# Moving the layer-norm preparation of the later MLP batches one chunk ahead of the matrix work (one core, 16 batches)

## The chip, the cores and the metric

The kernel runs on one core of a Trainium2 chip. The metric is the device time of one execution in microseconds; lower is better. The engines go by the profile's names: PE (matmuls) with PEld (its weight loads), DVE (vector), ACT (scalar, activations), POOL (GpSimd) and SP (which here only issues DMAs, one after the other in the order written).

## The reference, cut to what matters

A transformer block over 16 batches of 256 tokens with 256 features: self-attention, cross-attention, and then, for each batch, the MLP part, which is all that the change touches:

```
x_norm2 = modulate(_ln(x), shift_m, scale_m)     # _ln: over the 256 features of a token
h = jax.nn.gelu(x_norm2 @ W_mlp1 + b_mlp1)       # 256 -> 1024
h = h @ W_mlp2 + b_mlp2                          # 1024 -> 256
x = x + gate_m[:, None] * h
```

## The kernel before, in words

The attention of all batches runs first (some 560 us) and writes its result to a DRAM tensor `x2d`. Then a loop runs over `chunks`: 16 batches b with 4 chunks c each, i = 4b + c. A chunk is 256 of the 1024 hidden features. All matrix products are three fp32r matmuls in place of one (high part and low part of each factor), so a chunk is 12 matmuls into the hidden layer (`mlp_first`, PSUM tile `ph`) and 12 out of it (`mlp_second`, into the PSUM tiles `s` for even batches and `st` for odd ones).

In iteration i the PE does `mlp_first` of chunk i+2 and then `mlp_second` of chunk i-1. Between the two, ACT applies the gelu to chunk i+1 (`mlp_gelu`: twice `hf` and twice `hh`, from `ph`), and POOL subtracts (`hl` = `hf` - `hh`). There are two PSUM buffers for `ph`. So `mlp_first` of chunk i+2 cannot start before the gelu of chunk i has read its `ph`.

What a batch m needs before its own first chunk is prepared while earlier batches compute, in these steps:

1. `mlp_load(m)`: SP reads x of the batch from `x2d` (a DMA of 256 KB).
2. `mlp_bias(m)`: POOL adds a bias row, x <- x, cb.
3. `mlp_stats(m)`: DVE `BATCH_NORM_STATS2` (`st_m`) and aggregate (`mv_m`); `ln.pow()`: POOL makes the reciprocal deviation, two small instructions on `rs_m`.
4. `mlp_apply(m)`: DVE normalises in two instructions (`xn_m`) and transposes in blocks (`blk_m`); SP writes the blocks to a DRAM tensor `turned` in 4 DMAs.
5. `mlp_fetch(m)`: SP reads them back, regrouped, into `raw_m` in 4 DMAs, which wait for the 4 writes.
6. `mlp_T(m)`: ACT scales and shifts (`xTf_m` from `raw_m`, two instructions), POOL splits the result into a high part (a cast into `wkch` or `wqch`) and a low part (`wkcl` or `wqcl`). With that, `mlp_first(m, 0)` can run.

DVE also does the end of each batch: `mt` (PSUM times gate, waits for the last `mlp_second` of the batch), `y` (plus residual) and, a little earlier, `xmg`.

What sets the order: PE, DVE, POOL and SP keep the order in which the program is written. ACT keeps it only in the iterations i < 23; behind them (`ACT.on` is False) a scheduler, which works with estimated durations when the kernel is built, chooses the place of each ACT instruction. That concerns `xTf_m` from batch 7 on: it is written in iteration (m-1, 0), behind that iteration's gelu, but the scheduler puts it earlier. In the trace each engine runs its list in order, so an `xTf_m` that waits for its read back holds every gelu behind it.

Of the kernel before, what the change touches and what calls it, by code (L numbers as in the profile page):

```python
# [21 lines left out]
def pixart_block(  # L22
# [8 lines left out]
    B, N, H = x.shape  # L31
# [69 lines left out]
    def tok(ap, b):  # L101
        return ap[b].rearrange("(p t) h -> p t h", p=P)
# [329 lines left out]
    def mm3_tok(dst, xT, t, W, kn=KC, start=True, stop=True):  # L432
        n = 0
        for k in range(kn):
            for a, b in ((xT[0], W[0]), (xT[0], W[1]), (xT[1], W[0])):
                PE.matmul(dst, a[:, k, t * P:(t + 1) * P], b[:, k],
                          start=(start and n == 0), stop=(stop and n == 3 * kn - 1))
                n += 1
# [134 lines left out]
    def bc_t(ap):  # L573
        return ap.unsqueeze(1).to_broadcast([P, NT, H])
# [113 lines left out]
    def side(home, r):  # L688
        return home[r] if isinstance(home, (list, tuple)) else home[:, r]
# [111 lines left out]
    M = {}  # L801
# [9 lines left out]
    def mlp_bias(b):  # L811
        POOL.tensor_tensor(M[b].xt, M[b].xt, bc_t(cb), ALU.add)

    def mlp_stats(b, power=False):
        M[b].ln.steps[0]()
        M[b].ln.steps[1](power)

    BY_DVE = range(3, B)
    turned = dram.tile([2, 32, 16, 4, 32], F32, name="turned", bufs=1)

    def mlp_apply(b):
        m = M[b]
        if b not in BY_DVE:
            m.ln.steps[2]("dve")
            return
        xn = work.tile([P, 4, KC, NT, 32], F32, tag="xn", name=f"xn_m{b}", bufs=3)
        for t in range(NT):
            DVE.tensor_scalar(xn[:, :, :, t], m.xt[:, t].rearrange("p (f g c) -> p g f c", f=KC, g=4),
                              m.ln.mv[:, t, 0:1], m.ln.rs[:, t:t + 1], ALU.subtract, ALU.mult)
        blocks = work.tile([P, 4, KC * NT, 32], F32, tag="A", name=f"blk_m{b}", bufs=1)  # L830
        DVE.transpose(blocks.rearrange("p g x c -> p (g x c)"), xn.rearrange("p g f t c -> p (g f t c)"))
        home = turned[b % 2]
        for i in range(4):
            SP.dma_start(home[:, :, i], blocks[32 * i:32 * i + 32].rearrange("p g x c -> p (g x) c"))

    def mlp_fetch(b):
        m, home = M[b], turned[b % 2]
        m.raw = work.tile([P, KC, N], F32, tag="oT", name=f"raw_m{b}")
        for g in range(4):
            SP.dma_start(m.raw[32 * g:32 * g + 32].rearrange("p f n -> p (f n)"),  # L840
                         home[:, 4 * g:4 * g + 4].rearrange("a x i c -> a (x i c)"))
# [7 lines left out]
    def mlp_residual(b):  # L849
        m = M[b]  # L850
        m.xg = work.tile([P, NT, H], F32, tag="x1", name=f"xmg_{b}", bufs=7)
        DVE.tensor_tensor(m.xg, m.xt, bc_t(m.g[:, 1]), ALU.add)

    def mlp_T(b):

        m = M[b]
        raw = b in BY_DVE
        pst = m.raw.rearrange("p f n -> p (f n)") if raw else ps_gen(f"psT_m{b}", SHORT)
        for f in range(0 if raw else KC):
            for t in range(NT):  # L860
                PE.transpose(pst[:, f * N + t * P:f * N + (t + 1) * P],
                             m.ln.xn[:, t, f * P:(f + 1) * P], ident)
        y = work.tile([P, KC, N], F32, tag="y", name=f"xTf_m{b}", bufs=2)
        hi, lo = (Wkc, Wqc)[b % 2]
        if raw:
            for f in range(KC):
                ACT.activation(y[:, f], m.raw[:, f], AF.Identity,
                               bias=cpT[:, 6 + f, b:b + 1], scale=sc1[:, 1, f, b:b + 1])
            POOL.tensor_copy(hi, y)
            POOL.tensor_tensor(lo, y, hi, ALU.subtract)  # L870
            m.xT = (hi, lo)
            return
        for f in range(KC):
            DVE.tensor_scalar(y[:, f], pst[:, f * N:(f + 1) * N], sc1[:, 1, f, b:b + 1],
                              cpT[:, 6 + f, b:b + 1], ALU.mult, ALU.add)
        if b in E_['DV']:
            DVE.tensor_copy(hi, y)
        else:
            for f in range(KC):
                ACT.activation(hi[:, f], pst[:, f * N:(f + 1) * N], AF.Identity,  # L880
                               bias=cpT[:, 6 + f, b:b + 1], scale=sc1[:, 1, f, b:b + 1])
        DVE.tensor_tensor(lo, y, hi, ALU.subtract)
        m.xT = (hi, lo)
# [3 lines left out]
    def mlp_first(b, c):  # L887

        ph = ps_gen(f"ph_{b}_{c}", LONG).rearrange("p (j n) -> p j n", j=2)
        for j in range(2):  # L890
            mm3(ph[:, j], W1, 2 * c + j, M[b].xT)
        M[b].h[c] = ph
# [27 lines left out]
    def mlp_gelu(b, c):  # L920
        ph = M[b].h.pop(c)
        homes = (("pt", 5), ("qkh", 3), ("qkl", 3))
        if b == 0 and c:
            homes = (("x1", 7),) + (homes[1:] if c < 3 else (("xTh", 5), ("xTl", 5)))
        hf, hh, hl = [work.tile([P, 2, N], t, tag=tag, name=f"{n}_{b}_{c}", bufs=bufs)
                      for n, t, (tag, bufs) in zip(("hf", "hh", "hl"), (F32, F32R, F32R), homes)]
        for dst in (hf, hh):
            if c in M[b].kept:
                ACT.activation(dst, ph, AF.Gelu_apprx_tanh)
                continue  # L930
            for j in range(2):
                f = BM1 + 2 * c + j
                ACT.activation(dst[:, j], ph[:, j], AF.Gelu_apprx_tanh, bias=bT[:, f:f + 1])
        POOL.tensor_tensor(hl, hf, hh, ALU.subtract)
        M[b].hT[c] = (hh, hl)

    def mlp_second(b, c):
        m = M[b]
        hT = m.hT.pop(c)
        if c == 0:  # L940
            m.po = [side((sp, st)[b % 2], t)[:, :H] for t in range(NT)]
            if b == B - 1:
                m.po[1] = side(sp, 1)[:, :H]
        for t in range(NT):
            mm3_tok(m.po[t], hT, t, [W2[0][:, 2 * c:2 * c + 2], W2[1][:, 2 * c:2 * c + 2]],
                    kn=2, start=(c == 0), stop=(c == NCH - 1))
        if c == NCH - 1:
            t1 = work.tile([P, NT, H], F32, tag="t1", name=f"mt_{b}")
            y = work.tile([P, NT, H], F32, tag="x1", name=f"y_{b}", bufs=7)
            if b < B - 1:  # L950
                for t in range(NT):
                    DVE.tensor_tensor(t1[:, t], m.po[t], m.g[:, 0], ALU.mult)
                DVE.tensor_tensor(y, m.xg, t1, ALU.add)
                SP.dma_start(tok(out, b), y)
                return
            for t, q in enumerate((SP, ACT)):
                DVE.tensor_tensor(t1[:, t], m.po[t], m.g[:, 0], ALU.mult)
                DVE.tensor_tensor(y[:, t], m.xg[:, t], t1[:, t], ALU.add)
                q.dma_start(tok(out, b)[:, t], y[:, t])
# [106 lines left out]
    for i in range(3):  # L1066
        b = i if i < 2 else 0
# [191 lines left out]
    for i, (b, c) in enumerate(chunks):  # L1259
        ACT.on = i < E_['AP']  # L1260
        if 2 < i < len(chunks) - 1:
            mlp_gelu(*chunks[i + 1])
        if i in turns:
            mlp_T(turns[i])
        if c == 3 and b > 0 and b + 3 in BY_DVE:
            mlp_apply(b + 3)
        if c == 0 and b > 1 and b + 2 in BY_DVE:
            mlp_fetch(b + 2)
        if i in firsts:
            mlp_first(*chunks[firsts[i]])  # L1270
        if i > 0:
            mlp_second(*chunks[i - 1])
        for f in pst.get(i, ()):
            f()
        ahead = b + 2 if 2 < b + 2 < B else None
        soon = ahead if ahead and ahead in BY_DVE else None
        if c == 0 and ahead and not soon:
            mlp_bias(ahead)
        if c == 0 and b > 0 and b + 3 in BY_DVE:
            mlp_bias(b + 3)  # L1280
        if c == 1:
            if b + 1 < B:
                mlp_gates(b + 1)
            if b > 0 and b + 3 in BY_DVE:
                mlp_stats(b + 3)
                M[b + 3].ln.pow()
            if ahead and not soon:
                mlp_stats(ahead)
        if c == 2 and ahead and not soon:
            M[ahead].ln.pow()  # L1290
        if c == 0 and 4 < b + 4 < B:
            mlp_load(b + 4)
        if c == 3:
            if ahead and not soon:
                mlp_apply(ahead)
            mlp_residual(b)
    mlp_second(*chunks[-1])


# [46 lines left out]
```

## Time and profile before

| | |
|---|---|
| median of 3 runs | 736.87 us (735.96 to 737.25) |
| the profiled execution | 736.51 us, of which the span (first to last instruction) is 734.7 us |
| PE busy | 727.2 us, 99% of the span |
| DVE, ACT, POOL busy | 565.7, 562.8 and 521.5 us |
| granted PE clock | 0.999 on average |
| DMA queue of SP | 92.27 MB, 45.5% of 16 engines |

The MLP loop fills the last 170 us or so, from about 560 us on. In it the PE works through 12 matmuls in about 1.42 us, an iteration in 2.83 us and a batch in 11.33 us, as long as nothing makes it wait. Batch numbers in the trace follow from that raster: iteration (4, 0) starts at about 594.6 us, iteration (8, 0) at 640.88 us. The changes begin in iteration (2, 3), about 583 us.

### The profile page before, as it was taken

The numbers are of one execution on the slowest core, as the hardware profiler recorded it, in microseconds if no ns is written. First come the engines' busy times: TensorE is split into PE (matmuls) and PEld (weight loads), VectorE is DVE, ScalarE is ACT, GpSimd is POOL, SyncE is SP. The second block draws the span as 40 slices with busy tenths as digits, with TensorE's granted clock in tenths as the row PEclk, the third lists the DMA queues.
The fourth block names the chain that finished last, engine by engine and source line by source line (L and its number), as shares of the span: only waits on it lengthen the run. The fifth ranks groups of instructions, "written<-read, shape, count | busy, mean of one in ns | idle before, by whom it ended". The sixth has DMA issues, their size and how long they took to land.

```text
span 734.7 us, 25385 instructions
## 1 busy us (share of the span) xinstructions
PE 727.2 (99%) x10092; PEld 642.2 (87%) x10092; DVE 565.7 (77%) x1164; ACT 562.8 (77%) x976; POOL 521.5 (71%) x638
## 2 busy tenths in 40 slices
PE   9999999999999999999999999999999999999997
PEld 9778888888888888888888888888889999999997
DVE  4888888988888888988888889888746765556542
ACT  4277898888888888888888888888887666666663
POOL 6757576858567575856757687888576888898873
PEclk9999999999999999999999999999999999999999
DMA  6755444543545454354545456454321644444421
GB/s 209 203 149 146 130 134 137 141 125 96 154 115 155 131 142 136 107 152 114 159 125 143 137 145 161 124 158 129 117 74 36 164 133 113 112 124 100 116 80 37
DMA packets 108906, 94.81 MB, mean 129 GB/s; under 512 B 36914, under 2 KB 92756, under 8 KB 108788
## 3 DMA queue, kind: packets, MB, share of 16 engines
q1 hardware_dynamic: 108308, 92.27, 45.5%
q8 instruction: 80, 1.31, 0.8%
q0 software_dynamic: 192, 0.52, 0.3%
q10 hardware_dynamic: 288, 0.39, 0.2%
q14 instruction: 38, 0.31, 0.1%
HBM read 30.38 MB, written 11.86 MB: 57 GB/s over the span
## 4 chain that ended last, share of the span: by engine, by line
PE 90%; POOL 2%; DVE 2%; issue 2%; ACT 2%; DMA 1%; SPq 1%; ACTq 0%; POOLq 0%; DVEq 0%
PE s L51 17%; PE o L51 16%; PE st L51 14%; PE ph L51 8%; PE ps_q L51 5%; PE ps_qc L51 5%; PE ps_kc L51 4%; PE ps_P_s L51 3%; PE ps_v_c L51 3%; PE ps_k L51 3%; PE ps_v_s L51 2%; PE ps_P_c L51 2%; PE ps_h L51 1%; PE psT_q L51 1%; PE psA_c L51 1%
## 5 line engine op out<-in xcount | busy, mean ns | idle before, releaser
L51 DVE TENSOR_REDUCE mx<-s 128x2 f32<-128x512 f32 x504 | 324.4, 683 | 64.1 <-PE s L51 57.0
L51 ACT ACTIVATE pt<-st 128x1024 f32<-128x1024 f32 x252 | 259.0, 1028 | 16.6 <-PE st L51 10.8
L51 PE MATMUL s<-big 63*128 63x256 f32 (+1 forms) x1024 | 183.5, 297 | 0.2 <-DVE mx L51 0.2
L51 PEld LDWEIGHTS s<-big 63*128 63x128 f32 (+1 forms) x1024 | 133.2, 185 | 19.0 <-DVE l_kc L51 6.6
L51 PE MATMUL st<-big 64*128 64x256 f32 (+1 forms) x1024 | 133.8, 298 | 0.3 <-ACT pt L51 0.2
L51 PE MATMUL o<-pt,v 128*32 128x256 f32 x2048 | 123.8, 382 | 0.0
L51 PEld LDWEIGHTS st<-big 64*128 64x128 f32 (+1 forms) x1024 | 95.5, 185 | 16.2 <-issue 12.9
L51 POOL TENSOR_TENSOR hl<-hf,hh 128x512 fp32r<-128x512 f32 x64 | 85.4, 1342 | 32.3 <-ACT hh L51 31.9
L51 PEld LDWEIGHTS o<-pt,v 128*32 128x32 f32 x2048 | 60.2, 109 | 41.4 <-PE psm L51 0.2
L51 ACT ACTIVATE hh<-ph,bT 128x256 fp32r<-128x256 f32 x114 | 47.9, 472 | 23.2 <-PE s L51 10.9
L51 ACT ACTIVATE hf<-ph,bT 128x256 f32<-128x256 f32 x114 | 47.6, 471 | 21.6 <-PE ph L51 21.5
L51 ACT COPY oT<-o 128x512 f32<-128x512 f32 x63 | 37.0, 587 | 33.5 <-PE o L51 33.5
L51 PE MATMUL s<-big,hh 128*128 128x256 f32 x272 | 49.8, 282 | 0.0
L51 PE MATMUL ph<-wkch,wself 128*128 128x256 f32 x224 | 44.5, 282 | 0.5 <-ACT hh L51 0.4
L51 PE MATMUL ph<-wqch,wself 128*128 128x256 f32 x224 | 44.3, 281 | 0.0
L51 PE MATMUL ps_k<-xTh_s,wself 64*128 64x256 f32 (+1 forms) x232 | 43.9, 294 | 0.0
L51 PE MATMUL st<-big,hh 128*128 128x256 f32 x240 | 43.8, 281 | 0.0
L51 DVE TENSOR_SCALAR xn_m<-x,mv_m,rs_m 128x256 f32<-128x256 f32 x28 | 28.7, 1066 | 19.1 <-POOL rs_m L51 19.1
L51 POOL CAST xTh_c<-y_c 128x512 fp32r<-128x512 f32 x16 | 9.8, 613 | 45.5 <-ACT y_c L51 45.5
L51 PEld LDWEIGHTS s<-big,hh 128*128 128x128 f32 x272 | 41.4, 188 | 0.0
L51 PE MATMUL ps_q<-xTh_s,wself 64*128 64x256 f32 (+1 forms) x240 | 39.8, 283 | 0.4 <-DVE l_q L51 0.4
L51 PE MATMUL ps_v_s<-wself,xTh_s 64*128 64x256 f32 x224 | 39.2, 294 | 0.0
(249 smaller groups left out, 2496.1 us busy)
## 6 DMA issues: line engine op xcount, KB each, us to landing
big<-h_kc SPq DMA_DIRECT2D x64, 128.0 KB
big<-h_qc SPq DMA_DIRECT2D x64, 128.0 KB
big<-h_k SPq DMA_DIRECT2D x62, 128.0 KB
big<-h_q SPq DMA_DIRECT2D x62, 128.0 KB
big<-l_k SPq DMA_DIRECT2D x32, 128.0 KB
big<-l_q SPq DMA_DIRECT2D x32, 128.0 KB
g<-gd SPq DMA_DIRECT2D x16, 256.0 KB
c<-in_ctx_dram SPq DMA_DIRECT2D x16, 256.0 KB
```

What stands on the lines that cost most here:

```text
L51: i = f(*a, **k)
```

## The change

For batches m of 6 and above, four steps are written earlier:

| step | before, in iteration | now, in iteration |
|---|---|---|
| `mlp_bias(m)` | (m-3, 0) | (m-4, 3), at its end |
| `mlp_stats(m)` and `ln.pow()` | (m-3, 1) | (m-3, 0) |
| `mlp_apply(m)` | (m-3, 3) | (m-3, 2) |
| `mlp_fetch(m)` | (m-2, 0) | (m-3, 3) |

Nothing is added or removed, and `mlp_load` and `mlp_T` stay where they were written.

```diff
-        if c == 3 and b > 0 and b + 3 in BY_DVE:
+        if b > 0 and b + 3 in BY_DVE and c == (2 if b + 3 >= 6 else 3):
             mlp_apply(b + 3)
-        if c == 0 and b > 1 and b + 2 in BY_DVE:
+        if c == 3 and 6 <= b + 3 < B:
+            mlp_fetch(b + 3)
+        if c == 0 and 3 < b + 2 < 6:
             mlp_fetch(b + 2)
...
-        if c == 0 and b > 0 and b + 3 in BY_DVE:
+        if c == 0 and 3 < b + 3 < 6:
             mlp_bias(b + 3)
+        if c == 0 and 6 <= b + 3 < B:
+            mlp_stats(b + 3)
+            M[b + 3].ln.pow()
         if c == 1:
...
-            if b > 0 and b + 3 in BY_DVE:
+            if 3 < b + 3 < 6:
                 mlp_stats(b + 3)
                 M[b + 3].ln.pow()
...
             mlp_residual(b)
+            if 6 <= b + 4 < B:
+                mlp_bias(b + 4)
```

What it does to the engines' lists is seen in two places; the lists of DVE, SP and PE hold the same instructions in the same order as before.

ACT, around the last gelus of batch 5 (`hf_5_3` is the gelu of batch 5, chunk 3; `xTf_m7` belongs to `mlp_T(7)`), before:

```order
L51 ACTIVATE xTf_m6_13173<-raw_m6_13005,cpT_101,sc1_103 128x256 x2
L51 ACTIVATE hf_5_2_13217<-ph_5_2_13183,bT_104 128x256 x2
L51 ACTIVATE hh_5_2_13218<-ph_5_2_13183,bT_104 128x256 x2
L51 ACTIVATE hf_5_3_13261<-ph_5_3_13225,bT_104 128x256 x2
L51 ACTIVATE hh_5_3_13262<-ph_5_3_13225,bT_104 128x256 x2
L51 ACTIVATE xTf_m7_13346<-raw_m7_13178,cpT_101,sc1_103 128x256 x2
L51 ACTIVATE hf_6_0_13294<-ph_6_0_13269,bT_104 128x256 x2
L51 ACTIVATE hh_6_0_13295<-ph_6_0_13269,bT_104 128x256 x2
```

and now:

```order
L51 ACTIVATE xTf_m6_13179<-raw_m6_12965,cpT_101,sc1_103 128x256 x2
L51 ACTIVATE hf_5_2_13226<-ph_5_2_13184,bT_104 128x256 x2
L51 ACTIVATE hh_5_2_13227<-ph_5_2_13184,bT_104 128x256 x2
L51 ACTIVATE xTf_m7_13352<-raw_m7_13138,cpT_101,sc1_103 128x256 x2
L51 ACTIVATE hf_5_3_13261<-ph_5_3_13234,bT_104 128x256 x2
L51 ACTIVATE hh_5_3_13262<-ph_5_3_13234,bT_104 128x256 x2
L51 ACTIVATE hf_6_0_13303<-ph_6_0_13278,bT_104 128x256 x2
L51 ACTIVATE hh_6_0_13304<-ph_6_0_13278,bT_104 128x256 x2
```

The scheduler has put `xTf_m7` one gelu earlier, ahead of chunk 3 of batch 5 in place of chunk 0 of batch 6. The same holds for batches 8 to 15, nine in all; `xTf_m6` stays where it was.

POOL, in batch 6 (`x2_9` is the bias sum of batch 9, `rs_m9` its deviation), before:

```order
L51 TENSOR_TENSOR hl_6_0_13296<-hf_6_0_13294,hh_6_0_13295 128x512
L51 TENSOR_TENSOR hl_6_1_13340<-hf_6_1_13338,hh_6_1_13339 128x512
L51 CAST wqch_93<-xTf_m7_13346 128x512
L51 TENSOR_TENSOR wqcl_94<-xTf_m7_13346,wqch_93 128x512
L51 TENSOR_TENSOR x2_9_13215<-x2_9_13215,cb_106 128x512
L51 TENSOR_TENSOR hl_6_2_13392<-hf_6_2_13390,hh_6_2_13391 128x512
L51 TENSOR_SCALAR rs_m9_13431<-mv_m9_13428 128x2
L51 TENSOR_TENSOR rs_m9_13431<-rs_m9_13431,mhalf_73 128x2
L51 TENSOR_TENSOR hl_6_3_13436<-hf_6_3_13434,hh_6_3_13435 128x512
```

and now:

```order
L51 TENSOR_TENSOR hl_6_0_13305<-hf_6_0_13303,hh_6_0_13304 128x512
L51 TENSOR_TENSOR x2_9_13224<-x2_9_13224,cb_106 128x512
L51 TENSOR_TENSOR hl_6_1_13346<-hf_6_1_13344,hh_6_1_13345 128x512
L51 CAST wqch_93<-xTf_m7_13352 128x512
L51 TENSOR_TENSOR wqcl_94<-xTf_m7_13352,wqch_93 128x512
L51 TENSOR_SCALAR rs_m9_13394<-mv_m9_13391 128x2
L51 TENSOR_TENSOR rs_m9_13394<-rs_m9_13394,mhalf_73 128x2
L51 TENSOR_TENSOR hl_6_2_13401<-hf_6_2_13399,hh_6_2_13400 128x512
L51 TENSOR_TENSOR hl_6_3_13436<-hf_6_3_13434,hh_6_3_13435 128x512
```

The bias sum has moved from behind the split of batch 7 to ahead of `hl_6_1`, and the two `rs` instructions from behind `hl_6_2` to ahead of it.

## The prediction

> **What bounds the kernel now.** First the page's span and the busy time by stretches (columns: length, then busy time and count for PE, PEld, DVE, ACT and POOL, then granted clock, DMA share, GB/s), for the part in which the change acts:
>
> ```profile
> span 734.7 us, 25385 instructions
> ...
> core 0: us, PE busy (x) PEld busy (x) DVE busy (x) ACT busy (x) POOL busy (x), PEclk, DMA share, GB/s
> 580.00:600.00 20.00, 20.00 (x172) 20.00 (x171) 13.29 (x18) 13.56 (x33) 17.47 (x16) 1.00 0.51 129
> 600.00:620.00 20.00, 19.59 (x166) 19.39 (x165) 11.13 (x19) 12.86 (x32) 15.85 (x16) 1.00 0.48 130
> 640.00:660.00 20.00, 19.89 (x169) 19.69 (x167) 11.00 (x20) 13.33 (x34) 17.30 (x16) 1.00 0.45 117
> 660.00:680.00 20.00, 20.00 (x172) 20.00 (x171) 11.73 (x18) 13.84 (x34) 16.85 (x16) 1.00 0.42 105
> 720.00:734.70 14.70, 10.41 (x89) 10.20 (x87) 4.85 (x8) 4.20 (x10) 3.98 (x3) 0.94 0.11 38
> ```
>
> PE sets the pace: 172 matmuls in 20 us, one each 0.1163 us (0.118 by the raster of single rows). It loses time in two stretches only: 6 matmuls at 600 to 620 (0.70 us) and 3 at 640 to 660 (0.35 us), together 1.05 us. That is all that removing waits can bring. Then the waits from 580 to 720 (total, times, longest):
>
> ```profile
> DVE st_m L51 <- POOL x L51: 11.9, 10, 1.2
> ACT xTf_m L51 <- DMA raw_m<-turned: 11.1, 8, 2.7
> ...
> PEld ph L51 <- ACT hh L51: 0.9, 2, 0.6
> ```
>
> DVE's statistics wait 1.19 us in each batch for POOL's bias sum; ACT's `xTf_m` waits for the read back; and twice that reaches PE through `hh`. The first of these cases, batch 7, in the order in which the rows release each other (start, duration):
>
> ```profile
> 597.64 0.75 DVE L51 TENSOR_TENSOR mt<-st,gm 128x256 f32<-128x256 f32 x2 [1.65 <-PE st L51]
> 598.43 1.20 DVE L51 TENSOR_TENSOR y<-xmg,mt 128x512 f32<-128x512 f32 x1
> ...
> 599.05 1.73 POOL L51 TENSOR_TENSOR x<-x,cb 128x512 f32<-128x512 f32 x1
> ...
> 600.81 0.75 DVE L51 BATCH_NORM_STATS2 st_m<-x 128x6 f32<-128x256 f32 x2 [1.18 <-POOL x L51]
> ...
> 602.41 0.72 POOL L51 TENSOR_TENSOR rs_m<-rs_m,mhalf 128x2 f32<-128x2 f32 x1
> 603.10 2.61 POOL L51 TENSOR_TENSOR hl<-hf,hh 128x512 fp32r<-128x512 f32 x2
> ...
> 603.17 2.69 DVE L51 TENSOR_SCALAR xn_m<-x,mv_m,rs_m 128x256 f32<-128x256 f32 x2 [1.39 <-POOL rs_m L51]
> 605.89 0.71 DVE L51 STREAM_TRANSPOSE blk_m<-xn_m 128x512 f32<-128x512 f32 x1
> ...
> 606.63 2.57 SPq L51 DMA_DIRECT2D turned<-blk_m  x4
> ...
> 615.25 1.10 ACT L51 ACTIVATE xTf_m<-raw_m,cpT,sc 128x256 f32<-128x256 f32 x2 [2.66 <-DMA raw_m<-turned]
> ...
> 616.97 0.83 ACT L51 ACTIVATE hh<-ph,bT 128x256 fp32r<-128x256 f32 x2
> ...
> 617.85 0.38 PE L51 MATMUL ph<-wkch,wself 128*128 128x256 f32 x1 [0.41 <-ACT hh L51]
> ```
>
> The chain starts with `mt`, which PE releases at the end of batch 3, and ends 17.61 us later, when the read back lands and `xTf_m7` starts. From there to the released matmul it is 617.85 - 615.25 = 2.60 us (`xTf`, `hf`, `hh`). PE needs that gelu, chunk 0 of batch 6, for the matmuls of iteration (6, 0). `mt` starts 0.20 us behind the end of iteration (4, 0) on the raster, and seven iterations of 2.833 us (24 matmuls) lie between: 19.83 - 0.20 = 19.63 us. So the read back may land at most 19.63 - 2.60 = 17.03 us after `mt`. It was late by 0.58 us, and the matmul at 617.85 is 0.57 us behind the raster. The model holds to 0.01 us here.
>
> **The change, part by part.**
>
> 1. The bias sum ahead of `hl_1` takes away DVE's wait: statistics, deviation, normalising, write and read back come 1.19 us sooner. DVE and SP keep their lists, so moving `mlp_stats`, `mlp_apply` and `mlp_fetch` in the program does nothing more there: the next wait in line is `y`, then the DMAs' own time.
>
> 2. ACT's list is the cost. From batch 7 to 15 `xTf_m` stands one gelu earlier. The gelu now held up is chunk 3 of batch m-2, needed by PE one iteration, 2.83 us, sooner. The limit falls from 17.03 to 14.20 us, while the data gain 1.19 us.
>
> 3. The two `rs` ahead of `hl_2` let two `hl` run back to back while DVE normalises. With two, `xn` takes 2.69 us (above); with one:
>
> ```profile
> 649.62 1.29 POOL L51 TENSOR_TENSOR hl<-hf,hh 128x512 fp32r<-128x512 f32 x1
> ...
> 649.70 1.70 DVE L51 TENSOR_SCALAR xn_m<-x,mv_m,rs_m 128x256 f32<-128x256 f32 x2 [1.39 <-POOL rs_m L51]
> ```
>
> So it is 1 us (2.67 is the usual long value, I take 0.97) more where the second `hl` is ready in time: `hl_2` and `hl_3` now, the latter only if its gelu wasn't late, which is the case in a batch without a stall. [...]
>
> The other late landings, `mt` and `xTf` of batches 9, 11, 13 and 15:
>
> ```profile
> 620.99 0.42 DVE L51 TENSOR_TENSOR mt<-st,gm 128x256 f32<-128x256 f32 x1 [3.60 <-PE st L51]
> ...
> 638.28 1.10 ACT L51 ACTIVATE xTf_m<-raw_m,cpT,sc 128x256 f32<-128x256 f32 x2 [2.35 <-DMA raw_m<-turned]
> ...
> 644.02 0.42 DVE L51 TENSOR_TENSOR mt<-st,gm 128x256 f32<-128x256 f32 x1 [3.19 <-PE st L51]
> ...
> 659.79 0.60 ACT L51 ACTIVATE xTf_m<-raw_m,cpT,sc 128x256 f32<-128x256 f32 x1 [0.82 <-DMA raw_m<-turned]
> ...
> 666.69 0.42 DVE L51 TENSOR_TENSOR mt<-st,gm 128x256 f32<-128x256 f32 x1 [2.43 <-PE st L51]
> ...
> 682.75 0.60 ACT L51 ACTIVATE xTf_m<-raw_m,cpT,sc 128x256 f32<-128x256 f32 x1 [1.11 <-DMA raw_m<-turned]
> ...
> 689.36 0.42 DVE L51 TENSOR_TENSOR mt<-st,gm 128x256 f32<-128x256 f32 x1 [2.15 <-PE st L51]
> ...
> 704.81 0.60 ACT L51 ACTIVATE xTf_m<-raw_m,cpT,sc 128x256 f32<-128x256 f32 x1 [0.51 <-DMA raw_m<-turned]
> ```
>
> | batch | before | less 1.19 | plus 0.97 where `xn` was short | over 14.20 |
> |---|---|---|---|---|
> | 7 | 17.61 | 16.42 | 16.42 | 2.22 |
> | 9 | 17.29 | 16.10 | 16.10 | 1.90 |
> | 11 | 15.77 | 14.58 | 15.55 | 1.35 |
> | 13 | 16.06 | 14.87 | 15.84 | 1.64 |
> | 15 | 15.45 | 14.26 | 15.23 | 1.03 |
>
> The even batches fall between: a batch's chain lasts 1.5 batches, so a stall of PE for batch m gives batch m+1 that much more room, and with the gelu late its `xn` is short. The worst of them that I checked, batch 14:
>
> ```profile
> 678.02 0.42 DVE L51 TENSOR_TENSOR mt<-s,gm 128x256 f32<-128x256 f32 x1 [0.29 <-PE s L51]
> ...
> 694.52 0.60 ACT L51 ACTIVATE xTf_m<-raw_m,cpT,sc 128x256 f32<-128x256 f32 x1 [1.54 <-DMA raw_m<-turned]
> ```
>
> 16.50 - 1.19 = 15.31, over by 1.11, less than the 1.64 that batch 13 has given: no stall. Then batch 15 finds the gelu on time, and the pattern repeats every second batch, as at 617 and 641 in the trace of before.
>
> The sum: five stalls, 2.22 + 1.90 + 1.35 + 1.64 + 1.03 = 8.14 us; each restart costs 0.10 more (the first matmul lasts 0.38, the usual 0.28), 0.5; less the 1.05 that is lost today: +7.6 us. Against the profiled execution's own 736.51 that is 744.1 us (the median of the runs is 0.36 above it).
>
> 4. POOL's order at `hl_1`, cast and low part, costed at nothing:
>
> ```profile
> 595.67 1.48 POOL L51 TENSOR_TENSOR hl<-hf,hh 128x512 fp32r<-128x512 f32 x1 [1.15 <-ACT hh L51]
> ...
> 597.79 1.30 POOL L51 TENSOR_TENSOR wqcl<-xTf_m,wqch 128x512 fp32r<-128x512 f32 x1
> ...
> L51 PE MATMUL ph<-wqch,wself x184: 278/282/283, 600.3 to 721.6; 128*128 128x256 f32 x184
> ```
>
> The bias sum (1.73) fills an idle 1.15 us ahead of `hl_1` and pushes the rest by 0.6; the low part then ends near 599.7, and PE reads it first at 600.3. The cover is 0.6 us; beyond it every 0.1 us is PE's. `hl_2` behind `rs` starts near 0.2 to 1 us later than today and is needed over 2 us later.
>
> **The rivals.**
>
> - *The data land in time* (not slower). Place: `raw_m` at ACT. The shortest chain above less 1.19 is 14.26 us against 14.20; if less DMA work beside it (share 0.42 to 0.51 above) lets read backs land 1 to 2 us sooner, no stall is left and the 1.05 goes too: 735.5 us. It decides below 14.2 us after `mt`. Against it: five of five odd batches are over, four by a lot with the longer `xn`.
> - *`xn` keeps the length it had.* Then the odd batches are over by 2.22, 1.90, 0.38, 0.67 and 0.06, batch 14 by 1.11 - 0.67 = 0.44: 5.7 us, with restarts and less 1.05 about +5.2: 741.7 us. For it: ACT's wait delays `hl_3` whenever it is near the limit.
> - *The bias sum waits for its load.* x of batch 7 is issued here:
>
> ```profile
> 591.20 0.43 SPq L51 DMA_DIRECT2D x<-x2d  x1
> ```
>
> and read at 599.05 today, but near 594.6 now, with the issue about 1 us sooner: some 4 us for landing, where `raw_m` needs up to 4.4 us from its first issue. Late by 1 us it costs PE 0.4 (cover 0.6) in nine batches, partly taken from the stalls above: about 747 us.
> - *The clock drops after a stall.* In the row 720 to 734.7, with 4.3 us idle, the clock is 0.94: 0.06 x 14.7 = 0.9 us; five times is +4.4, 748.5 us. Against it: 1.00 in the rows with stalls. [...]
>
> **How the numbers follow.** 0.2% (1.5 us) is about what a measurement of this kernel can tell from no change. Long `xn` and alternating stalls 0.57, slower; short `xn` 0.20 (0.18 slower, 0.02 within); data in time 0.15 (0.10 within; 0.05 faster, since more than the 1.05 us at hand would have to come from elsewhere); late load 0.05 and clock 0.03, slower. Slower 0.83, within 0.12, faster 0.05. The likeliest gives 744.1, with its own range 741 to 747: landings vary by about 1 us, and five count. The range over the cases: if batches 7 and 9 land as batch 15 did (1.03 each) and `xn` stays short in the others (1.11 together), it is 2.06 + 1.11 + 0.5 - 1.05 = +2.6, 739.1; I take 738.0, a third of the way from there to the data in time. At the top, 0.8 us longer landings in all five stalls give 748.1; I take 748.0. This leaves out most of the first rival and the worst of the last.
>
> **What the profile after would show.** Right: `DVE st_m <- POOL x` gone; `xTf_m <- DMA` waits of 2 to 5 us ahead of chunk 3; PE waiting 1 to 2.2 us for `hh` in every second batch, at the start of the last iteration of batches 5, 7, 9, 11 and 13 (near 614, 639, 663, 687 and 711 us); `xn` of 2.7 us in the batches without a stall. Wrong: no PE waits from 590 to 720 (first rival), stalls in the first two only (second), or POOL waiting for a DMA at x (third). A read back that starts much sooner than 11 to 12 us after `mt` would overthrow the sum.

## The result and the profile after

The changed kernel takes 744.68 us (median of 5 runs, 742.88 to 745.04), the kernel before on the same chip 736.78 us (735.69 to 737.25): ratio 1.0105, 95% interval 1.0093 to 1.0116. It is slower by about 7.9 us; 744.1 was forecast. The profiled execution took 744.84 us. Its span, and the stretches of the changed part (columns as before: length, busy time and count of PE, PEld, DVE, ACT, POOL, then granted clock, DMA share, GB/s):

```profile
span 743.0 us, 25385 instructions
...
580.00:600.00 20.00, 19.32 (x164) 19.12 (x163) 12.39 (x19) 12.76 (x31) 16.91 (x17) 1.00 0.51 132
600.00:620.00 20.00, 18.48 (x156) 18.28 (x155) 12.93 (x22) 12.41 (x30) 15.50 (x15) 1.00 0.51 127
640.00:660.00 20.00, 18.44 (x157) 18.23 (x156) 10.29 (x16) 14.12 (x34) 15.96 (x15) 1.00 0.45 116
660.00:680.00 20.00, 19.37 (x164) 19.16 (x163) 11.99 (x21) 12.54 (x31) 15.52 (x16) 1.00 0.42 119
```

PE does 156, 157 and 164 matmuls where it did 166, 169 and 172, at the same full clock: it stands still more. What it stands still for is in the waits from 580 to 730 of the changed kernel (total in us, times, longest):

```profile
ACT xTf_m L51 <- DMA raw_m<-turned: 20.2, 9, 3.8
...
PEld ph L51 <- ACT hh L51: 6.5, 5, 1.8
PE ph L51 <- ACT hh L51: 5.5, 5, 1.6
...
DVE st_m L51 <- POOL x L51: 1.2, 1, 1.2
PEld ph L51 <- POOL wkcl L51: 0.9, 1, 0.9
POOL x L51 <- DMA x<-x2d: 0.8, 1, 0.8
```

DVE's statistics no longer wait for POOL: once in place of ten times, the one left being batch 5, which the change leaves alone. But ACT now waits 20.2 us for the read back in place of 11.1, and PE five times for `hh`. Batch 7's chain from `mt` (DVE) to `xTf` (ACT), the two ends of batch 9's, the `xn` of batches 7 and 8, and the five stalls of PE (the matmuls that start behind them):

```profile
600.12 0.76 DVE L51 TENSOR_TENSOR mt<-st,gm 128x256 f32<-128x256 f32 x2 [2.97 <-PE st L51]
...
604.48 2.68 DVE L51 TENSOR_SCALAR xn_m<-x,mv_m,rs_m 128x256 f32<-128x256 f32 x2 [1.15 <-POOL rs_m L51]
...
614.90 1.70 DVE L51 TENSOR_SCALAR xn_m<-x,mv_m,rs_m 128x256 f32<-128x256 f32 x2 [1.42 <-POOL rs_m L51]
...
616.00 1.09 ACT L51 ACTIVATE xTf_m<-raw_m,cpT,sc 128x256 f32<-128x256 f32 x2 [3.77 <-DMA raw_m<-turned]
...
618.60 0.39 PE L51 MATMUL ph<-wkch,wself 128*128 128x256 f32 x1 [1.52 <-ACT hh L51]
...
624.57 0.76 DVE L51 TENSOR_TENSOR mt<-st,gm 128x256 f32<-128x256 f32 x2 [6.65 <-PE st L51]
...
640.50 1.09 ACT L51 ACTIVATE xTf_m<-raw_m,cpT,sc 128x256 f32<-128x256 f32 x2 [3.82 <-DMA raw_m<-turned]
...
643.10 0.39 PE L51 MATMUL ph<-wkch,wself 128*128 128x256 f32 x1 [1.56 <-ACT hh L51]
...
666.67 0.39 PE L51 MATMUL ph<-wkch,wself 128*128 128x256 f32 x1 [0.63 <-ACT hh L51]
...
690.80 0.39 PE L51 MATMUL ph<-wkch,wself 128*128 128x256 f32 x1 [1.18 <-ACT hh L51]
...
714.36 0.39 PE L51 MATMUL ph<-wkch,wself 128*128 128x256 f32 x1 [0.63 <-ACT hh L51]
```

Batch 7 lands 616.00 - 600.12 = 15.88 us after `mt`, 1.68 over the limit of 14.20, and the released matmul starts 2.60 us behind `xTf`, as before the change. Batch 9 lands 640.50 - 624.57 = 15.93 us after its `mt`. On the raster of PE (a half iteration every 1.417 us) the five stalls are 1.67, 1.72, 0.79, 1.34 and 0.79 us: 6.31. (The figure in brackets is 0.16 less, because the profile has the last matmul before the gap take 0.28 us, where the raster gives it 0.118.) All five lie at the start of the last iteration of batches 5, 7, 9, 11 and 13, and between them, for the even batches' `xTf`, there is none. `xn` alternates between 2.7 and 1.7 us, as forecast.

There is a sixth stall, earlier, that the sum did not hold:

```profile
582.42 0.44 SPq L51 DMA_DIRECT2D x<-x2d  x1
...
586.45 1.30 POOL L51 TENSOR_TENSOR x<-x,cb 128x512 f32<-128x512 f32 x1 [1.60 <-PE ph L51]
...
590.10 1.28 POOL L51 TENSOR_TENSOR wkcl<-xTf_m,wkch 128x512 fp32r<-128x512 f32 x1
...
591.43 0.39 PE L51 MATMUL ph<-wkcl,wself 128*128 128x256 f32 x1 [0.68 <-POOL wkcl L51]
```

The bias sum of batch 6 starts 4.03 us after the issue of its load and has idled 1.60 us. The profile names PE as releaser, but the sum reads nothing of PE's; in the repeat of this order (below) the same row names the load. The split behind it is late, and PE loses 0.94 us.

Together, with 0.11 us for each of five restarts: 6.31 + 0.55 + 0.94, less the 1.05 that was lost before, is +6.75. The rest of the difference of the spans (743.0 - 734.7 = 8.3) is not in the MLP. The same early matmul, ahead of everything changed, in the kernel before and in the changed one:

```profile
551.41 0.39 PE L51 MATMUL psP_c<-wcph,xTh_ac 128*128 128x256 f32 x1
```

```profile
552.96 0.39 PE L51 MATMUL psP_c<-wcph,xTh_ac 128*128 128x256 f32 x1
```

It starts 1.55 us later. From this matmul to the end of the span it is 183.29 us before and 190.04 after, a difference of 6.75. This length is used below to compare traces, since it leaves the start-up out.

### The profile page after: what moved, and what is told of

It reads as the page before. It is cut to its first block, busy times and chain, and to the rows that moved or that the text cites. A ratio compares the mean times of both kernels' runs of the same rounds, so it can differ in the third digit from the quotient of the medians.

```text
span 743.0 us, 25385 instructions
## 1 busy us (share of the span) xinstructions
PE 729.7 (98%) x10092; PEld 642.7 (86%) x10092; DVE 568.7 (77%) x1164; ACT 562.2 (76%) x976; POOL 518.6 (70%) x638
## 4 chain that ended last, share of the span: by engine, by line
PE 86%; ACT 3%; DVE 3%; DMA 3%; issue 3%; SPq 2%; POOL 1%; ACTq 0%; DVEq 0%; POOLq 0%
PE s L51 16%; PE o L51 16%; PE st L51 14%; PE ph L51 7%; PE ps_qc L51 5%; PE ps_q L51 4%; PE ps_kc L51 3%; PE ps_P_s L51 3%; PE ps_v_s L51 3%; PE ps_k L51 3%; PE ps_v_c L51 3%; PE ps_P_c L51 2%; SPq L51 2%; DMA raw_m<-turned 1%; PE ps_h L51 1%
## 5 line engine op out<-in xcount | busy, mean ns | idle before, releaser
L51 DVE TENSOR_SCALAR xn_m<-x,mv_m,rs_m 128x256 f32<-128x256 f32 x28 | 32.8, 1212 | 17.8 <-POOL rs_m L51 17.8
L51 PEld LDWEIGHTS ph<-wkch,wself 128*128 128x128 f32 x224 | 36.3, 189 | 6.5 <-ACT hh L51 6.5
```

Source lines behind the costliest of these rows:

```text
L51: i = f(*a, **k)
```

## The experiments

The variants write `xTf` out by hand: ACT keeps the written order in the whole loop, and the two activations of `mlp_T` stand at a stated place. The edit, with K and C for the place ("early", K = 2 and C = 3, is the place that the scheduler chose in the changed kernel, ahead of the gelu of chunk 3 of batch m-2; "late", K = 1 and C = 0, is the one it chose before, ahead of chunk 0 of batch m-1; "written" is behind the gelu of chunk 1 of batch m-1, where the program has `mlp_T`, and has only the first added line):

```diff
-        ACT.on = i < E_['AP']
+        ACT.on = True
+        if i + 1 < len(chunks):
+            gb, gc = chunks[i + 1]
+            if gc == C and 7 <= gb + K < B:
+                mlp_T_act(gb + K)          # the two activations of mlp_T
         if 2 < i < len(chunks) - 1:
             mlp_gelu(*chunks[i + 1])
```

Every time is the median; the ratio is to runs of the kernel before beside it on the same chip (their own medians lay between 736.58 and 737.76); the length is from the `psP_c` matmul to the end in the profiled execution, one for each kernel.

| kernel | ACT's `xTf` | POOL's order | us | ratio (95%) | length |
|---|---|---|---|---|---|
| before | late | old | 736.78 | | 183.29 |
| changed | early | new | 744.68 | 1.0105 (1.0093 to 1.0116) | 190.04 |
| a1 | late | new | 737.40 | 1.0000 (0.9984 to 1.0015) | 183.35 |
| a2 | early | old | 753.25 | 1.0204 (1.0177 to 1.0231) | 197.98 |
| a3 | written | new | 737.26 | 0.9988 (0.9972 to 1.0005) | 183.44 |
| a4 | written | old | 736.23 | 0.9979 (0.9962 to 0.9995) | 182.27 |
| b0 | early | new | 743.80 | 1.0107 (1.0083 to 1.0132) | 190.49 |
| b1 | early | bias sum new, `rs` old | 739.55 | 1.0046 (1.0033 to 1.0059) | 185.91 |
| b2 | written | new, bias sums of 6 and 7 old | 736.72 | 1.0000 (0.9990 to 1.0009) | 183.14 |
| d1 | early | new, without `hl_2` | 738.58 | 1.0035 (1.0023 to 1.0047) | 184.97 |
| a5 (a4 again) | written | old | 736.49 | 0.9997 (0.9988 to 1.0007) | 182.27 |

**The two halves of the change.** DVE, SP and PE have the same lists before and after, so the change is ACT's slot and POOL's order. a1 has POOL's new order alone (the changed kernel with the late slot), a2 ACT's early slot alone.

> The changed kernel with one thing undone: ACT keeps the place of xTf that it had before (ahead of chunk 0 of batch m-1, for batches 7 to 15), written out; POOL, DVE, SP and PE as in the changed kernel. Theory S (the slot of xTf on ACT is the cost): the limit for the read back is again 17.03 us after mt, and the chains of the changed kernel (16.1 to 17.0 us in its trace) stay under it, so PE waits for hh nowhere from 600 us on; what is left is the one wait of 0.9 us for the low part of batch 4, which comes from the bias sum of batch 6 waiting for its load. Against 1.05 us of waits before: 736.4 to 737 us, ratio 0.999 to 1.001. Theory P (the bias sum and rs ahead of the hl on POOL are the cost): it stays at 742 to 744 us.

> The kernel before with one thing added: ACT's xTf of batches 7 to 15 stands where the changed kernel has it (ahead of chunk 3 of batch m-2); POOL, DVE, SP and PE as before. Theory S: the limit falls to 14.20 us while nothing comes sooner; by the landings of the trace before the odd batches are late by 3.4, 3.1, 1.6, 1.9 and 1.3 us, 11.2 in all, with 0.1 for each restart and less the 1.05 us that is lost today +10.6 us: 746 to 749 us, slower than the changed kernel, ratio about 1.014. Theory P: POOL's order is untouched, so 736 to 738 us.

a1 is as fast as the kernel before, with no stall of PE but the one near 590 us (0.98). So with the late slot POOL's order is worth nothing on balance (it brings that stall and takes away the 1.05 us of the kernel before), and the slot is the cost. a2 shows the slot alone, and it is dearer than forecast: +15 us. Its gaps of PE sum up to 10.45 us on the raster (11.2 were expected): four long ones, one of 0.97 and a last one of 0.2. The rest is the clock. The four long gaps (the released matmul of each), and the stretches behind two of them:

```profile
617.67 0.39 PE L51 MATMUL ph<-wkch,wself 128*128 128x256 f32 x1 [2.46 <-ACT hh L51]
...
644.10 0.39 PE L51 MATMUL ph<-wkch,wself 128*128 128x256 f32 x1 [1.97 <-ACT hh L51]
...
694.68 0.39 PE L51 MATMUL ph<-wkch,wself 128*128 128x256 f32 x1 [2.04 <-ACT hh L51]
...
719.77 0.39 PE L51 MATMUL ph<-wkch,wself 128*128 128x256 f32 x1 [2.16 <-ACT hh L51]
```

```profile
645.80:648.30 2.50, 2.50 (x13) 2.50 (x13) 0.00 (x0) 0.84 (x2) 1.05 (x1) 0.50 0.30 52
...
694.60:697.00 2.40, 2.32 (x19) 2.32 (x20) 0.00 (x0) 2.09 (x7) 2.13 (x2) 1.00 0.48 85
```

After the gap of 1.97 us the granted clock is 0.50 and 13 matmuls take 2.50 us; after that of 2.04 it stays at 1.00. The raster is late by 1.6 us after each of the gaps of 2.46, 1.97 and 2.16, beside the gap itself. 10.45 of gaps, 4.87 of three clock falls and the remaining restart, 0.3 in all, less 1.05, is +14.6; the length says +14.69.

**The written order.**

> The changed kernel with ACT kept in the order in which the program is written to the end: xTf of batch m behind chunk 1 of batch m-1, two gelus later than in the kernel before. Theory S: no read back is late for that place; only the 0.9 us at batch 4 is left: 736.2 to 737 us. Theory P: 742 to 744 us. A rival within S: xTf is now so late that cast and low part on POOL reach PE late; then PE waits for wkcl or wqcl in every batch, which would show as such.

> The kernel before with ACT kept in written order to the end; everything else as before. Theory S: its two waits of PE for hh (1.05 us) go and nothing else changes: 735.4 to 736 us, ratio 0.998 to 0.999. If the late place of xTf makes cast and low part late, PE waits for them instead and the time is 737 or more.

In a4 PE has no stall in the whole MLP, and its length is 1.02 less than before the change: the 1.05 that the kernel before loses to its own early `xTf`. By time it was 0.9979. Repeated:

> The kernel before with xTf in ACT's written order once more: the first time 0.9979 of the kernel before, interval 0.9962 to 0.9995, which is at the edge of what can be told. Its MLP has no PE stall; the kernel before loses 1.05 us to two. Theory S: 1.0 us less, ratio 0.9985. Rival (the first ratio was chance): 1.000.

Again there is no stall and the length is 182.27, but the ratio is 0.9997, interval 0.9988 to 1.0007: the value of the rival, with 0.9985 outside. 1 us is less than runs of this kernel can tell, with the start differing by as much between executions (the `psP_c` matmul starts at 551.83 in the one and 552.43 in the other). In the trace it beats the kernel before by 1 us; by the times of the runs that isn't shown.

**The term of the longer `xn`.** d1 leaves out the subtraction `hl_2` (the low part of chunk 2) in the batches from 4 on; PE reads the low part of chunk 1 in its place:

```diff
+        if c == 2 and 3 < b:
+            M[b].hT[c] = (hh, M[b].hl1)
+            return
...
         POOL.tensor_tensor(hl, hf, hh, ALU.subtract)
         M[b].hT[c] = (hh, hl)
+        M[b].hl1 = hl if c == 1 else None
```

> The changed kernel, with ACT's early slot, but POOL leaves out the low part (hl) of chunk 2 in the batches from 4 on, and PE reads the low part of chunk 1 in its place, so PE's work and waits for data stay the same. Now no second hl runs beside DVE's normalising. Theory S (the longer xn, +0.97 us, is a term of the stalls): xn takes 1.70 us or less in every batch; the five chains of the changed kernel (15.88, 15.93, 15.00, 15.55, 14.99 us after mt) become 14.91, 14.96, 14.03, 14.58, 14.02, over the limit of 14.20 by 0.71, 0.76, 0, 0.38 and 0; stalls 1.85 in place of 6.31 us, so 5 us less than the changed kernel: 739 to 741. Rival (short and long xn end in the same landing, since the write and the read back wait for something else): 743 to 745 as the changed kernel.

b1 keeps all work, and puts only `rs` back behind `hl_2`:

```diff
         if c == 0 and 6 <= b + 3 < B:
             mlp_stats(b + 3)
+        if c == 1 and 6 <= b + 3 < B:
             M[b + 3].ln.pow()
```

> The changed kernel, with ACT's early slot and the bias sum early, but the two rs instructions back behind hl_2 on POOL, as before the change. This divides POOL's reordering in two. Theory S: the bias sum is what gives back the 1.2 us, so the kernel stays close to the changed one; POOL idles 1.5 us ahead of rs in the changed kernel, and hl_2 would fill that idle time, so rs comes about 0.5 us later, and xn is 0.5 to 1 us shorter: chains 0 to 0.5 shorter, 741 to 745. Rival (moving rs ahead is what gives back the time): as the kernel with the early slot alone, 750 to 754.

Both are 5 to 6 us under the changed kernel, 738.58 and 739.55 us; by the ratios, which leave out differences between occasions, 5.2 and 4.3. d1 lies a little under its range, and b1 beats what either theory expected of it. The groups of `xn` from 580 to 730, of the changed kernel and of b1 (busy time, mean ns of one | idle time before them):

```profile
L51 DVE TENSOR_SCALAR xn_m<-x,mv_m,rs_m 128x256 f32<-128x256 f32 x22 | 25.5, 1200 | 14.1 <-POOL rs_m L51 14.1
```

```profile
L51 DVE TENSOR_SCALAR xn_m<-x,mv_m,rs_m 128x256 f32<-128x256 f32 x22 | 14.0, 676 | 17.5 <-POOL rs_m L51 17.5
```

The same 22 instructions take 14.0 us in place of 25.5, 1.05 us less for each batch. And `rs` hardly comes later for it (of the POOL list around batch 10, the changed kernel and b1):

```profile
649.08 1.30 POOL L51 TENSOR_TENSOR wqcl<-xTf_m,wqch 128x512 fp32r<-128x512 f32 x1
651.89 0.22 POOL L51 TENSOR_SCALAR rs_m<-mv_m 128x2 f32<-128x2 f32 x1 [1.52 <-DVE mv_m L51]
```

```profile
647.19 1.74 POOL L51 TENSOR_TENSOR hl<-hf,hh 128x512 fp32r<-128x512 f32 x1
649.01 0.22 POOL L51 TENSOR_SCALAR rs_m<-mv_m 128x2 f32<-128x2 f32 x1
649.32 0.72 POOL L51 TENSOR_TENSOR rs_m<-rs_m,mhalf 128x2 f32<-128x2 f32 x1
650.00 1.29 POOL L51 TENSOR_TENSOR hl<-hf,hh 128x512 fp32r<-128x512 f32 x1
```

In the changed kernel POOL idles 1.52 us for the aggregate, and both `hl` come when `xn` runs. In b1 `hl_2` fills that idle time and one `hl` or none is left beside `xn`. `rs` starts 2.82 us after `mt` in the changed kernel (`mt` at 649.07) and 3.04 in b1 (at 645.97), 0.2 later for about 1 us less of `xn`. Batch 7's chain is 14.61 us in b1 and 14.46 in d1, where the changed kernel has 15.88. Not all of a shorter `xn` arrives: in batches 9 and 13 of b1 it is 1.95 and 1.94 us shorter, but the landing comes only 0.99 and 0.57 us sooner. There the reads are issued 5.88 and 5.72 us behind the first write, in place of 5.19 and 4.55; why is open.

So the parts are: the early slot alone +15 us; with the bias sum ahead of `hl_1` (b1) +3.4 by the ratio; with `rs` ahead of `hl_2` too (the changed kernel) +7.7. The bias sum gives back nearly 12 of the 15, partly because b1's gaps, 0.88 us of idle PE or less, leave the clock at 1.00 where a2's three falls cost 4.87, and moving `rs` costs 4.3.

**The stall near 590 us.** b2 leaves the bias sums of batches 6 and 7 at their old place:

```diff
-        if c == 0 and 3 < b + 3 < 6:
+        if c == 0 and 3 < b + 3 < 8:
             mlp_bias(b + 3)
...
-            if 6 <= b + 4 < B:
+            if 8 <= b + 4 < B:
                 mlp_bias(b + 4)
```

> The changed kernel with xTf in ACT's written order, and with the bias sums of batches 6 and 7 left where they were before the change (behind the split), all later ones early. Theory L (the one stall left in that variant, 1.09 us near 589 us, is the bias sum of batch 6 waiting for the load of x, which holds the split behind it on POOL): no PE stall is left, 1.0 us less than that variant's 737.26: 736.0 to 736.6. Rival (the stall is that of the split itself, late for another reason): 737.0 to 737.8.

The stall at 590 is gone, and another of 0.8 us, with its restart, has come at 613 us, where the old place and the new follow each other and POOL's list runs over:

```profile
613.59 0.39 PE L51 MATMUL ph<-wkcl,wself 128*128 128x256 f32 x1 [0.54 <-POOL wkcl L51]
```

The total is no less, 736.72 (ratio 1.0000, where a3 has 0.9988), and it lies between the two expectations. The run shows that the early bias sum makes the stall at 590; it doesn't show that the load alone does. That the load was what came last there is read from the list and from b0's row, next.

**The changed kernel once more.** b0 has the lists of the changed kernel, with ACT's order written out:

> The instruction lists of the changed kernel on every engine, only with ACT's order written out in place of chosen by the scheduler: the anchor for the variants. Theory S: the same stalls at the same places (five of 0.8 to 1.7 us and one of 0.94 near 590 us), ratio to the kernel before 1.009 to 1.012; the start of the MLP on the time of the kernel before again, since the 1.5 us by which it came later in the profile of the changed kernel is a difference between executions: span 741 to 742. Rival (the change also costs 1.5 us ahead of the MLP): start of the MLP 1.5 us later again, span 743.

```profile
580.82 0.43 SPq L51 DMA_DIRECT2D x<-x2d  x1
585.57 1.30 POOL L51 TENSOR_TENSOR x<-x,cb 128x512 f32<-128x512 f32 x1 [2.15 <-DMA x<-x2d]
...
590.54 0.39 PE L51 MATMUL ph<-wkcl,wself 128*128 128x256 f32 x1 [0.96 <-POOL wkcl L51]
```

743.80 us, ratio 1.0107; the `psP_c` matmul starts at 551.51 again, and the span is 742.0. So the 1.5 us at the start were not the change's. Its stalls are 1.13, 1.72, 0.74, 1.81 and 0.71, and at 590 us 1.49 with a load that took 4.75 us.

**The clock.** After a2, two runs of a4's order with added activations on a spent tile ahead of the gelu of chunk 2, in numbers that differ by batch (9 to 14 in c1, 5 to 8 in c2), so that PE stands still for times of different length. A fall is a granted clock of 0.50 in place of 1.00:

```diff
+        if c == 1:
+            for _ in range({7: 5, 8: 6, 9: 7, 10: 8, 11: 7, 12: 8, 13: 6, 14: 7}.get(b, 0)):
+                ACT.activation(M[b].y[:, 1], M[b].y[:, 1], AF.Identity, ...)
         if 2 < i < len(chunks) - 1:
             mlp_gelu(*chunks[i + 1])
```

> The kernel before with xTf in ACT's written order (no PE stall in the MLP), and in batches 7 to 14 9, 10, 11, 12, 13, 14, 11 and 10 added activations of 128x256 on a spent tile, written ahead of the gelu of chunk 2. Each takes about 0.5 us, the first 6 fit into ACT's idle time, so PE should stand still for about 1.4, 1.9, 2.4, 2.9, 3.4, 3.9, 2.4 and 1.9 us, once per batch, with PE busy between. Theory H (a gap of some 2 us is enough for the granted clock to fall, as in the kernel with the early slot alone, where gaps of 2.1 to 2.6 us were followed by rows at 0.50 to 0.68): no fall at 1.4 to 1.9, a fall at 2.4 and more. [...] Each fall costs about 1.6 us beside the gap itself. Total 736 + 20 + falls: 758 to 768.

> The graded delay once more with fewer added activations: 5, 6, 7, 8, 7, 8, 6 and 7 in batches 7 to 14. In the first try each took 0.63 us, 9 of them gave a gap of 3.45 us, and all six gaps seen (3.45 to 6.6) were followed by some 3 us at half clock. At that price the gaps now are 0.93, 1.56, 2.19, 2.82, 2.19, 2.82, 1.56 and 2.19 us. Theory H (some 2 us are enough): clock 1.00 after 0.93 and 1.56, a fall after most gaps of 2.19 and all of 2.82, each with 1.6 us more: 735 + 16 + 6 to 8 = 757 to 760. [...]

c1 (792.23 us, one run) missed its range: the activations took 0.63 us each and found no idle time to hide in, the gaps were 3.29 us of idle PE and more, and a stretch at half clock followed each of the eight. c2 (754.99 us, one run) has gaps of 0.76 to 2.67 us of idle PE. The two longest, each with a stretch behind it:

```profile
676.82 0.36 PE L51 MATMUL ph<-wqch,wself 128*128 128x256 f32 x1 [2.66 <-ACT hh L51]
...
706.23 0.36 PE L51 MATMUL ph<-wqch,wself 128*128 128x256 f32 x1 [2.67 <-ACT hh L51]
```

```profile
678.80:681.00 2.20, 2.20 (x12) 2.20 (x12) 1.78 (x3) 0.84 (x2) 1.59 (x2) 0.50 0.00 0
...
706.20:710.00 3.80, 3.77 (x32) 3.80 (x33) 1.41 (x2) 2.90 (x8) 3.44 (x4) 1.00 0.06 17
```

2.66 us: a fall. 2.67 us: none. Three gaps of 2.03 and 2.04 us and three shorter ones: none. So theory H fails in c2. Over all MLP loops traced here, no gap up to 1.65 us was followed by a fall, of those from 1.97 to 2.67 us four in nine were, and all eight from 3.29 us on.

So the length alone does not decide; the place does. In the traces' record of the clock a fall lasts 3.41 us (6.83 after the three longest gaps of c1), and the falls of one trace start whole multiples of 3.413 us apart: in a2 at 618.12, 645.42 and 720.52 us, which is 8 and 22 of them. Here the time is cut on that raster (columns: length, busy time and count of PE, granted clock, DMA share, GB/s), the first two rows in a2, the others in c2:

```profile
642.01:645.42 3.41, 1.44 (x13) 1.00 0.53 162
645.43:648.83 3.40, 3.40 (x19) 0.50 0.31 59
...
660.73:664.14 3.41, 1.55 (x13) 1.00 0.77 231
664.15:667.55 3.40, 3.40 (x31) 1.00 0.04 11
...
701.69:705.10 3.41, 1.86 (x16) 1.00 0.60 193
705.11:708.51 3.40, 2.28 (x19) 1.00 0.17 42
```

The gap of 1.97 us lies in one stretch whole, and the next runs at half clock. That of 2.03 leaves 1.86 us of idle PE in one stretch, that of 2.67 is parted into 1.55 and 1.12: no fall. In the 13 traces, from 565 us on, no stretch at full clock with up to 1.86 us of idle PE was followed by a fall, and all 22 with 1.97 us or more were, counting those at the ends of the traces. (Near 35 us, in the attention, five traces show a fall with no idle PE ahead of it, in the changed kernel at 35.55 us behind a stretch of 3.41 us that PE fills; this does not explain them.)

## Why the prediction was right, and where it was not

- **ACT's slot is the cost** (step 2): right. The limit fell by one iteration, and the five chains exceed 14.20 by 1.68, 1.73, 0.80, 1.35 and 0.79, which are the stalls to 0.01 us. a1 and a2 show it from both sides.
- **The bias sum gives back 1.19 us a batch** (step 1): right in the wait, which is gone. Its worth is more than the 1.19: without it (a2) the gaps reach 2 us and the clock falls three times.
- **The longer `xn`** (step 3): right in the pattern. The second rival (`xn` keeps the length it had) gave 741.7 and did not come; d1 and b1 show the price of the longer `xn`, 4 to 5 us of the total. What was not seen: with no `hl` beside it `xn` takes 0.73 us, not 1.70, and one place later for `rs` would have saved the second `hl` for 0.2 us. Where there are two `hl`, `xn` ends 0.15 us behind the last (605.86 and 605.71 in the rows of batch 7 that the prediction shows); in its row of one `hl` it ends 0.49 behind (651.40 and 650.91).
- **The sum**: 8.14 us of stalls were forecast and 6.31 measured. The term that was too large is the chain: 16.42, 16.10, 15.55, 15.84 and 15.23 were forecast, 15.88, 15.93, 15.00, 15.55 and 14.99 came. Two parts of it differ. The start of `xn` behind `mt` was taken as 1.19 us sooner in all five; it came 1.17, 1.79, 1.79, 1.26 and 1.49 us sooner, about 0.25 of it because `xn` waits 1.15 for `rs` in place of 1.39, since POOL now stands ready at `rs`. And the DMAs' part, from the transpose `blk_m` to `xTf`, was taken as unchanged; it was 0.55 us shorter in batch 7 (8.81 in place of 9.36), 0.22 shorter in batch 13, 0.40 longer in batch 9 and within 0.06 in the others, for no reason that the runs show.
- **POOL's order at nothing** (step 4): wrong by 0.94 us in one batch. It is the mechanism of the third rival, which the prediction tied to batch 7 and to all nine. It came in batch 6, the first one; x of batch 7 waited 0.8 us without a stall of PE.
- **The clock**: it stayed at 1.00, for the stalls stayed at 1.56 us of idle PE or less. The sum held no fall for stalls of up to 2.22 us, and what the trace of before showed for that was two short ones (0.70 and 0.35 us); a2's gaps of 1.97 and 2.16 us were each followed by a fall. With stalls as long as forecast, 2.22 in batch 7 (2.06 of idle PE), the fourth rival could have come true, by the place of the gap on the clock's raster. One of six executions of b0, without a trace, took 749.74 us at a mean clock of 0.992.
- **The total**: stalls that were 1.83 us too large and an unforecast 0.94 leave the MLP at +6.75 to +7.2 (the changed kernel's profile and b0's), where +7.6 was forecast; the median of the runs says +7.9. So that 744.1 lies 0.6 us from the 744.68 measured is partly luck: the two errors had opposite signs, and something outside the traced stalls made up the rest. These 0.7 to 1.15 us between the traces and the runs are open: the start-up of single executions differs by up to 1.7 us (`psP_c` at 551.41 to 553.12 in the traces here), and no run tells whether that averages out.

## What to carry to other kernels

When preparation is moved earlier in the program, look at what each engine's list becomes: here the data of the five odd batches landed 0.5 to 1.7 us sooner, but the one instruction that waits for them went 2.8 us sooner, ahead of a gelu that PE needs, and an engine that runs its list in order then stands still for both (ACT for up to 3.8 us). On an engine with room to spare, place the waiting instruction late, at the last point that its own reader allows; in the written order (a3, a4) PE has no stall from it. Before putting a small instruction ahead of a big one on a helper engine, see whether it would wait there: the big one may fit into that wait, and otherwise it can run beside work that it slows (here `xn`, 2.67 us with two `hl` beside it in place of 0.73).

## What the runs showed of the hardware

- `xn` on DVE (two instructions, 128x256 each) takes 0.73 us alone (b1), 1.70 with one `hl` of POOL beside it and 2.67 with two (both in the changed kernel). Each of the two takes 0.40 us by itself, and about 1.38 where a `hl` has begun just ahead of it: it then ends 0.15 us behind that `hl`.
- On a raster of 3.41 us, whose phase differs from execution to execution (stretches begin at 618.12 us in a2 and at 664.15 in c2, 13.5 lengths apart), the granted clock fell to 0.50 for the next stretch after each stretch at full clock from 565 us on in which PE idled 1.97 us or more, and after none in which it idled 1.86 us or less. Such a fall costs about 1.6 us (a2, 4.87 for three). A gap between 1.97 and 2.67 us made it fall in four of nine cases (a2 and c2), by its place.
- A load of 256 KB was read 4.0 to 4.75 us after its issue where it came last (batch 6, in the changed kernel and b0).
- Activations in place on one tile, each reading the one before, follow each other every 0.63 us (c1, 9 in 5.67 us).
